# Relational graph layers on one core: engine order written out in the source, and the relation products dealt out between chunks

## The chip, the core and the metric

The kernel runs on one core of a Trainium2 chip. A core has a matrix engine, TensorE (PE in the profile, its weight loads PEld), three engines for elementwise work, VectorE (DVE), ScalarE (ACT) and GpSimd (POOL), and SyncE (SP), which here only issues transfers. Each engine takes its instructions in order; semaphores make it wait for others. SBUF is the working memory with 128 partitions, PSUM the memory that TensorE writes, in banks of 512 fp32 per partition. Transfers are issued by SP, ACT and POOL; the indirect ones, which gather rows by index, are issued by POOL.

The metric is the device time of one execution in microseconds, the median over runs, lower is better.

## The reference

6250 nodes with 256 features; 106250 edges, sorted by destination (each of 50000 pairs in both directions, and a loop at each node); 8 edge types; three relational layers, then one attention layer.

```
h = relu(layernorm(x))
for l in range(3):
    xr  = einsum('nd,rde->rne', h, W_rel[l])
    agg = segment_sum(xr[edge_type, src], dst)
    h   = relu(agg + h @ W_root[l] + bias[l])
x = x + h
h = relu(layernorm(x)) @ Wv + bv
c = leaky_relu((h @ wq + bq)[src] + (h @ wk + bk)[dst])
x = x + segment_sum(h[src] * softmax_over_dst(c), dst)
```

## The kernel before

The kernel looks at the edges and takes one of two paths; with these inputs it is `ordered_path`, which uses that edges are sorted by destination.

**Preparation.** Edges are cut into 831 chunks of 128. The nodes, then, are covered by 56 windows of consecutive chunks: 47 windows of 15 chunks (`CW`), then 9 of 14. A window's destinations fit into 128 nodes that begin at `base[t]`. The first loop (`groups`, four tiles of 128 nodes) normalizes x and writes two tables to memory: `xf[0]`, fp32 rows of h, and `tab[0]`, the same rows as three bf16 parts (high, middle, low) whose sum is the fp32 number: 768 bf16 per row. Each layer writes the next layer's `xf` and `tab`.

**A layer.** For a chunk, `gather` (L719) fetches the 128 source rows of `tab[l]` into `msg` (36 buffers). VectorE makes `hot` (L871): a row per edge with a single 1 at column 8 x (node in window) + type, over those nodes only that the chunk can reach (`ranges`, 104 to 336 columns). TensorE multiplies msg by hot (L852): for each half h of the features and each of the three parts, a weight load of 128 x 128 msg and a matmul into the PSUM banks of the window. There are four banks, two halves of 64 nodes times two halves of features, from a pool of five. A chunk that reaches over the middle needs two matmuls per weight load: 108 matmuls in a window of 15, 102 in one of 14. The last chunk of the window before is added once more with `hot_p`, 8 columns wide, for the node that is cut by the border.

**Finishing a window.** `finish_window` (L772) is called for window t-1 after chunk 2 of window t, and after the last window. It reads the window's own rows `xt` from `xf[l]` (`at_base`, L723, computes a register value from the base and the last hot, so that the load is not issued too early), copies the four banks to `ag` (three copies on ScalarE, L784, one on VectorE, L782), turns xt by two fp32 transposes into `pt` and copies it (L767, L769), and forms `po`: 16 products of `ag` with `W_rel` (L790, weight operand read with a step of 8 elements, since columns are ordered node by node with the type innermost) and two of xt with `W_root` (L793). An fp32 product appears in the profile as two instructions, so these are 32 and 4. Then come the bias (L795), relu and the split into three bf16 parts (L798, and `split`, L649), and stores to `tab[l+1]` and `xf[l+1]` (L801, L802). In the third layer, instead, x is added, stored as `xa`, normalized, turned (L767), multiplied by `Wv` (L818) and stored as a row of `hx`. `pt` and `po` have one PSUM buffer each.

**Attention.** It goes through the same windows and gathers rows of `hx` (L719 again, `head`, 48 buffers). The change does not touch it.

**What sets the order.** The kernel is written as one program; a scheduler decides in what order each engine gets its instructions, from what they need and from their buffers, and adds the semaphores. The next layer's gathers wait until all rows of its table are stored. The names that the change touches are `xf`, `base`, `hots`, `at_base`, `finish_window`, `turned_rows`, the loads at L742 to L751, and the loop at L833.

Of the kernel before, what the change touches and what calls it, by code (L numbers as in the profile page):

```python
# [10 lines left out]
F32 = mybir.dt.float32  # L11
BF16 = mybir.dt.bfloat16
I32 = mybir.dt.int32
# [416 lines left out]
def kernel(  # L430
# [52 lines left out]
    xf = [dram.tile([N + P, D], F32, name=f"xf{i}") for i in range(L)]  # L483
# [8 lines left out]
    base = keep.tile([1, NW], F32)  # L492
    last_i = keep.tile([P, 1], I32)
# [8 lines left out]
    with tc.tile_pool(name="prep", bufs=1) as prep, \  # L502
# [49 lines left out]
        for at, view, k in by_window(dst_t):  # L552
# [4 lines left out]
                              dst_t[0:1, CL + CW - 2:NC - (CW - 1):CW - 1])  # L557
        ones = prep.tile([1, P], F32)
# [109 lines left out]
    with tc.tile_pool(name="nw", bufs=3) as nw:  # L668
        zero = nw.tile([P, D], F32, bufs=1)
        nc.gpsimd.memset(zero, 0.0)  # L670
        nc.scalar.dma_start(xf[0][N:N + P, :], zero)
        for ts in groups:
            n = len(ts)
            xt = nw.tile([P, 4, D], F32, name="xt")
            whole = rows(ts[-1]) == P
            if whole:
                nc.sync.dma_start(
                    xt[:, :n, :],
                    x[ts[0] * P:(ts[-1] + 1) * P, :].rearrange("(t p) d -> p t d", p=P))
            else:  # L680
                nc.gpsimd.memset(xt, 0.0)
                for i, t in enumerate(ts):
                    nc.sync.dma_start(xt[:rows(t), i, :], x[t * P:t * P + rows(t), :])
            mv, rstd = statistics(nw, xt, n)
            for i in range(n):
                nc.vector.tensor_scalar(xt[:, i, :], xt[:, i, :], mv[:, i, 0:1],
                                        rstd[:, i:i + 1], op0=ALU.subtract, op1=ALU.mult)
            h0 = nw.tile([P, 4, D], F32, name="h0")
            nc.scalar.activation(h0[:, :n, :], xt[:, :n, :], AF.Relu)
            hml = nw.tile([P, 4, 3, D], BF16, name="hml")  # L690
            nc.scalar.copy(hml[:, :n, 0, :], h0[:, :n, :])
            nc.vector.tensor_sub(xt[:, :n, :], h0[:, :n, :], hml[:, :n, 0, :])
            nc.scalar.copy(hml[:, :n, 1, :], xt[:, :n, :])
            nc.gpsimd.tensor_sub(hml[:, :n, 2, :], xt[:, :n, :], hml[:, :n, 1, :])
            if whole:
                r0, r1 = ts[0] * P, (ts[-1] + 1) * P
                nc.sync.dma_start(xf[0][r0:r1, :].rearrange("(t p) d -> p t d", p=P),
                                  h0[:, :n, :])
                nc.sync.dma_start(tab[0][r0:r1, :].rearrange("(t p) w -> p t w", p=P),
                                  hml[:, :n].rearrange("p t s d -> p t (s d)"))  # L700
            else:
                for i, t in enumerate(ts):
                    nc.sync.dma_start(xf[0][t * P:t * P + rows(t), :], h0[:rows(t), i, :])
                    nc.sync.dma_start(tab[0][t * P:t * P + rows(t), :],
                                      hml[:rows(t), i].rearrange("p s d -> p (s d)"))

    def ordered_path():
# [23 lines left out]
        with ExitStack() as s:  # L731
            wp = s.enter_context(tc.tile_pool(name="weights", bufs=2))
            mp = s.enter_context(tc.tile_pool(name="msgs", bufs=36))
            op = s.enter_context(tc.tile_pool(name="hots", bufs=20))
# [4 lines left out]
            ops = s.enter_context(tc.tile_pool(name="ops", bufs=1, space=PSUM))  # L739

            wv_s = one.tile([P, KH, D], F32)
            nc.scalar.dma_start(wv_s, wv.rearrange("(k p) e -> p k e", p=P))  # L742
# [3 lines left out]
            for to, of in ((bv_s, bv), (wq_s, wq), (wk_s, wk)):  # L746
                nc.scalar.dma_start(to, rows_bcast(of, D))
            bq_s = one.tile([P, 1], F32)
            bk_s = one.tile([P, 1], F32)
            for to, of in ((bq_s, bq), (bk_s, bk)):  # L750
                nc.scalar.dma_start(to, rows_bcast(of, 1))  # L751
# [12 lines left out]
            def turned_rows(a: bass.AP, func):  # L764
                pt = ops.tile([P, KH, P], F32, name="pt")
                for k in range(KH):
                    nc.tensor.transpose(pt[:, k, :], a[:, k * P:(k + 1) * P], ident)  # L767
                at = rp.tile([P, KH, P], F32, name="at")
                nc.scalar.activation(at, pt, func)  # L769
                return at  # L770

            def finish_window(l: int, t: int, banks, hot, weights):  # L772

                wr, wo, bb = weights
                at = at_base(t, hot)
                xt = rp.tile([P, D], F32, name="xt")
                nc.sync.dma_start(xt, xf[l][ds(at, P), :])
                ag = ap_.tile([P, KH, 2, SEG // 2], F32, name="ag")
                for half in range(2):
                    for h in range(KH):  # L780
                        if half and h:
                            nc.vector.tensor_copy(ag[:, h, half, :], banks[half][h])  # L782
                        else:
                            nc.scalar.copy(ag[:, h, half, :], banks[half][h])  # L784
                x_t = turned_rows(xt, AF.Copy)
                po = ops.tile([P, D], F32, name="po")
                for r in range(R):
                    for h in range(KH):
                        by_r = ag[:, h].rearrange("p b (n r) -> p r (b n)", r=R)
                        nc.tensor.matmul(po, by_r[:, r, :], wr[:, h, r, :],  # L790
                                         start=(r == 0 and h == 0), stop=False)
                for h in range(KH):
                    nc.tensor.matmul(po, x_t[:, h, :], wo[:, h, :], start=False,  # L793
                                     stop=(h == KH - 1))
                nc.vector.tensor_add(po, po, bb)  # L795
                if l + 1 < L:
                    xs = rp.tile([P, D], F32, name="xs")
                    nc.scalar.activation(xs, po, AF.Relu)  # L798
                    hml = rp.tile([P, 3, D], BF16, name="hml")
                    split(hml, po, po, "relu")  # L800
                    nc.sync.dma_start(tab[l + 1][ds(at, P), :], hml.rearrange("p s d -> p (s d)"))  # L801
                    nc.sync.dma_start(xf[l + 1][ds(at, P), :], xs)  # L802
                    return
# [7 lines left out]
                nc.sync.dma_start(xa[ds(at, P), :], x1[:, 0, :])  # L811
                mv, rstd = statistics(rp, x1, 1)
                nc.vector.tensor_scalar(x1[:, 0, :], x1[:, 0, :], mv[:, 0, 0:1], rstd[:, 0:1],
                                        op0=ALU.subtract, op1=ALU.mult)
                h_t = turned_rows(x1[:, 0, :], AF.Relu)
                ph = ops.tile([P, D], F32, name="po")
                for h in range(KH):
                    nc.tensor.matmul(ph, h_t[:, h, :], wv_s[:, h, :], start=(h == 0),  # L818
                                     stop=(h == KH - 1))
                nc.vector.tensor_add(ph, ph, bv_s)  # L820
# [9 lines left out]
                nc.sync.dma_start(hx[ds(at, P), :], row)  # L830

            weights = load_weights(0)
            for l in range(L):  # L833
                nxt = load_weights(l + 1) if l + 1 < L else None
                ahead = None
                pending = None
                for t in range(NW):
                    n = sizes[t]
                    banks = [[gps.tile([P, SEG // 2], F32, name="bank") for _ in range(KH)]
                             for _ in range(2)]  # L840
                    begun = [False, False]
# [18 lines left out]
                    if ahead is not None:  # L860
                        hot = op.tile([P, R], BF16, name="hot_p", bufs=3)
                        nc.vector.tensor_scalar(hot, up[:, :R], seg_p[:, t:t + 1], None,
                                                op0=ALU.is_equal)
                        add(ahead, hot, 0, R)
                    for k in range(n):
                        c = first_c[t] + k
                        lo, hi = ranges[n][k]
                        msg = mp.tile([P, 3, D], BF16, name="msg")
                        gather(msg.rearrange("p s d -> p (s d)"), tab[l], src_t[:, c:c + 1])
                        hot = op.tile([P, WMAX], BF16, name="hot")  # L870
                        nc.vector.tensor_scalar(hot[:, :R * (hi - lo)], up[:, :R * (hi - lo)],  # L871
                                                seg[:, c:c + 1], None, op0=ALU.is_equal)
                        add(msg, hot, R * lo, R * hi)
                        ahead = msg
                        if k == 2 and pending is not None:
                            finish_window(l, *pending, weights)
                            pending = None
                    pending = (t, banks, hot)
                finish_window(l, *pending, weights)
# [116 lines left out]
```

## Time and profile before

| | |
|---|---|
| median of 3 runs, without a profiler | 4491.3 us (4487.84 to 4492.17) |
| profiled execution | 6330.7 us |
| its span | 6328.4 us |
| granted TensorE clock, mean over the span | 0.818 |
| first gather of layers 1, 2, 3 and of the attention | 146.9, 1651.9, 3142.0, 4628.9 us |
| gathers | 2493 in the layers, 831 in the attention, 0.945 us busy each |
| DMA, mean over the span | 116 GB/s |

The profile's times are those of one execution, the one with the profiler attached. It is much longer than the runs, so a row's mean duration can be taken from it, but not without care the time between rows.

```profile
PE   0687887888688788888868888888844454445545
PEld 0566666666566666666757777777733343334434
...
PEclk5788988888788888888878888888966677667767
DMA  5544444444344444444344444444422222222221
```

Each column is 1/40 of the span, each digit the busy share in tenths. The layers fill the first 29 columns, the attention the rest.

In the groups of the profile, the part after the bar is the busy time of a group in us with the mean of one in ns; after the next bar is the idle time of its engine just before it, and whose work ended that wait. "issue" there means that the engine waited for nothing that the profile shows.

### The profile page before, as it was taken

What the parts mean: (1) busy time and instruction counts of PE and PEld (TensorE: products, weight loads), DVE (VectorE), ACT (ScalarE), POOL (GpSimd) and SP (SyncE); (2) the same over time, 40 slices, a digit from 0 to 9 for tenths busy, and PEclk for the clock granted to TensorE, in tenths of its full rate; (3) what the DMA queues carried; (4) which work ended last, traced back from release to release, by engine and by line L of the source; (5) the groups of instructions that cost most, each with busy time, mean ns of one, the idle gap of its engine ahead of it and who ended that gap; (6) DMA issues with size and microseconds to landing.
All of it is one profiled execution on the core that took longest, in us unless ns stands there. A gap on an engine that the chain in (4) does not pass through costs nothing. (4 is left out here: it accounts for less than half of the span.)

```text
span 6328.4 us, 79952 instructions
## 1 busy us (share of the span) xinstructions
PE 4369.9 (69%) x29260; PEld 3685.4 (58%) x29260; DVE 2154.2 (34%) x6241; ACT 1153.1 (18%) x2566; POOL 3175.4 (50%) x3411
## 2 busy tenths in 40 slices
PE   0687887888688788888868888888844454445545
PEld 0566666666566666666757777777733343334434
DVE  5222322223232222323223333333323433334434
ACT  2011111111011111111101111111123333333333
POOL 2555555555355555555355555555444444444443
PEclk5788988888788888888878888888966677667767
DMA  5544444444344444444344444444422222222221
GB/s 181 150 130 129 134 128 131 129 124 136 114 130 128 129 132 132 131 130 135 103 137 134 134 134 135 133 135 138 123 71 74 71 73 78 76 73 73 78 75 53
DMA packets 327774, 732.72 MB, mean 116 GB/s; under 512 B 65165, under 2 KB 181059, under 8 KB 327372
## 3 DMA queue, kind: packets, MB, share of 16 engines
q0 software_dynamic: 199536, 599.93, 34.4%
q1 hardware_dynamic: 117512, 118.48, 5.8%
q10 hardware_dynamic: 10324, 9.11, 0.5%
q8 instruction: 232, 3.80, 0.3%
q14 instruction: 170, 1.39, 0.1%
HBM read 652.42 MB, written 74.88 MB: 115 GB/s over the span
## 5 line engine op out<-in xcount | busy, mean ns | idle before, releaser
L719 POOL DMA_INDIRECT msg<-tab,src_t x2493 | 2355.8, 945 | 2062.7 <-PE bank L852 1060.1
L852 PE MATMUL bank<-hot,msg 128*128 128x104 bf16 (+16 forms) x17982 | 1725.4, 252 | 582.1 <-issue 416.9
L852 PEld LDWEIGHTS <-msg 128*128 128x128 bf16 x18972 | 1418.5, 102 | 896.7 <-issue 699.0
L790 PE MATMUL po<-wr,ag 128*128 128x256 f32 x5376 | 1533.4, 446 | 183.8 <-issue 165.4
L790 PEld LDWEIGHTS po<-wr,ag 128*128 128x128 f32 x5376 | 1381.2, 335 | 327.0 <-issue 226.5
L871 DVE TENSOR_SCALAR hot<-up,seg 128x104 bf16<-128x104 f32 (+10 forms) x2493 | 1017.0, 431 | 1398.9 <-PE bank L852 972.0
L719 POOL DMA_INDIRECT head<-hx,src_t x831 | 785.5, 945 | 895.6 <-PE po L945 452.8
L920 PE MATMUL pq<-ident,qm 128*128 128x128 f32 x886 | 221.9, 342 | 679.4 <-ACT qm L918 293.4
L784 ACT COPY ag<-bank 128x512 f32<-128x512 f32 x504 | 284.9, 587 | 1887.8 <-PE bank L852 1085.3
L920 PEld LDWEIGHTS pq<-ident,qm 128*128 128x128 f32 x886 | 130.6, 158 | 753.8 <-ACT qm L918 328.0
L795 DVE TENSOR_TENSOR po<-po,bb 128x256 f32<-128x256 f32 x168 | 72.7, 433 | 1270.7 <-PE po L793 1247.2
L945 PE MATMUL po<-head,ex 128*128 128x256 f32 x1772 | 457.3, 416 | 42.6 <-issue 30.6
L945 PEld LDWEIGHTS po<-head,ex 128*128 128x128 f32 x1772 | 368.3, 214 | 111.3 <-issue 41.3
L924 DVE TENSOR_REDUCE tops<-pq 128x1 f32<-128x512 f32 x224 | 153.0, 683 | 553.3 <-ACT c L923 340.2
L918 ACT ACTIVATE qm<-other,head 128x128 f32<-128x128 f32 x886 | 298.7, 394 | 119.5 <-issue 95.9
L938 PE MATMUL pe<-ident,c 128*128 128x128 f32 x886 | 190.6, 388 | 152.3 <-ACT c L933 142.7
L938 PEld LDWEIGHTS pe<-ident,c 128*128 128x128 f32 x886 | 162.5, 205 | 174.4 <-ACT c L933 158.5
L911 DVE TENSOR_SCALAR other<-up,loc 128x128 f32<-128x128 f32 x831 | 256.9, 340 | 11.1 <-ACT qm L918 10.8
L923 ACT ACTIVATE c<-pq,sm 128x512 f32<-128x512 f32 x224 | 150.1, 683 | 572.6 <-remote 472.2
L798 ACT ACTIVATE xs<-po 128x256 f32<-128x256 f32 x112 | 42.9, 383 | 988.8 <-DVE po L795 980.1
L818 PE MATMUL po<-wv_s,at 128*128 128x256 f32 x224 | 111.8, 652 | 159.6 <-ACT at L769 156.0
L782 DVE COPY ag<-bank 128x512 f32<-128x512 f32 x168 | 116.1, 691 | 273.6 <-remote 128.7
(135 smaller groups left out, 1844.2 us busy)
## 6 DMA issues: line engine op xcount, KB each, us to landing
msg<-tab,src_t POOLq DMA_INDIRECT x2493
xt<-xf SPq DMA_DIRECT2D x168, 128.0 KB
tab<-hml SPq DMA_DIRECT2D x112, 192.0 KB
xf<-xs SPq DMA_DIRECT2D x112, 128.0 KB
head<-hx,src_t POOLq DMA_INDIRECT x831
tab<-hml SPq DMA_DIRECT2D x12, 768.0 KB
hx<-row SPq DMA_DIRECT2D x56, 128.5 KB
xa<-x SPq DMA_DIRECT2D x56, 128.0 KB
```

The source lines that it names most:

```text
L719: nc.gpsimd.indirect_dma_start(out=to, out_offset=None, in_=table[:N, :], in_offset=bass.IndirectOffsetOnAxis(ap=index, axis=0))
L784: nc.scalar.copy(ag[:, h, half, :], banks[half][h])
L790: nc.tensor.matmul(po, by_r[:, r, :], wr[:, h, r, :], start=(r == 0 and h == 0), stop=False)
L852: nc.tensor.matmul(banks[b][h][:, a - b * SEG // 2:z - b * SEG // 2], w, hot[:, a - lo:z - lo], start=(not begun[b] and s_ == 0), stop=Fal ...
L871: nc.vector.tensor_scalar(hot[:, :R * (hi - lo)], up[:, :R * (hi - lo)], seg[:, c:c + 1], None, op0=ALU.is_equal)
L911: nc.vector.tensor_scalar(other, up[:, :P], refs[j][1], None, op0=ALU.not_equal)
L918: nc.scalar.activation(qm, other, AF.Identity, scale=MASKED, bias=refs[j][0][:, D:HX])
L920: nc.tensor.transpose(pq[:, i, :], qm, ident)
L923: nc.scalar.activation(to, flat, AF.Identity, scale=SLOPE, bias=k2)
L924: nc.vector.tensor_reduce(tops[:, g:g + 1], flat, AX.X, ALU.max)
L938: nc.tensor.transpose(pe[:, i, :], c_t[:, j * P:(j + 1) * P], ident)
L945: nc.tensor.matmul(po, ex[:, i, :], refs[j][0][:, :D], start=(j == 0), stop=(j == len(refs) - 1))
```

## The change

- A call of `manual_schedule` at the start of the layers: each engine's instructions stay in the order in which the source gives them.
- `xf` is gone. The window's own rows are read from `tab[l]` as three bf16 parts, at chunk 4 of the window, at an address from `base_i`, an integer copy of `base`. They are turned by six bf16 matmuls with an identity `ident_b` that add the three parts up.
- `hot` has 10 buffers for 20 and is made five chunks ahead (`make_hot`).
- A half's two banks are allocated when its first chunk comes, and are copied out by ScalarE as soon as its last chunk is summed (`evacuate`). The copy reorders: `ag` is now [128, 2, type, node], so a product's weight operand is contiguous, and the read from PSUM has a step of 8 elements.
- `finish` is a generator. After each chunk it is resumed once, and issues its next piece: the turn; then 12 pieces of the 18 products (8 in the last layer); then bias, split and store, or in the last layer the norm, the turn, the product with `Wv` and the row, one piece each. A window's pieces are issued during the next window's chunks; what is left after the last chunk of a layer is run through at once, window after window.
- The loads for the head (`wv_s` and so on) are issued at the start of the third layer instead of the first.

```diff
-            op = s.enter_context(tc.tile_pool(name="hots", bufs=20))
+            s.enter_context(tc.manual_schedule())
+            op = s.enter_context(tc.tile_pool(name="hots", bufs=10))
...
+            def evacuate(banks, half: int, ag: bass.AP):
+                for h in range(KH):
+                    nc.scalar.copy(ag[:, h, :, half * (P // 2):(half + 1) * (P // 2)],
+                                   banks[half][h].rearrange("p (n r) -> p r n", r=R))
+            def finish(l: int, at, xt: bass.AP, ag: bass.AP, weights, t: int):
+                wr, wo, bb = weights
                 pt = ops.tile([P, KH, P], F32, name="pt")
                 for k in range(KH):
-                    nc.tensor.transpose(pt[:, k, :], a[:, k * P:(k + 1) * P], ident)
...
+                    for i in range(3):
+                        nc.tensor.matmul(pt[:, k, :], xt[:, i, k * P:(k + 1) * P], ident_b,
+                                         start=(k == 0 and i == 0), stop=(k == KH - 1 and i == 2),
+                                         skip_group_check=True)
+                x_t = rp.tile([P, KH, P], F32, name="x_t")
+                nc.scalar.copy(x_t, pt)
+                yield
+                last = l + 1 == L
+                parts = STEPS - (6 if last else 2)
+                todo = [(r, h) for r in range(R) for h in range(KH)] + [(R, h) for h in range(KH)]
+                po = ops.tile([P, D], F32, name="po")
+                done = 0
+                for i in range(parts):
+                    upto = len(todo) * (i + 1) // parts
+                    for r, h in todo[done:upto]:
+                        if r < R:
+                            nc.tensor.matmul(po, ag[:, h, r, :], wr[:, h, r, :],
+                                             start=(r == 0 and h == 0), stop=False,
+                                             skip_group_check=True)
                         else:
...
+                            nc.tensor.matmul(po, x_t[:, h, :], wo[:, h, :], start=False,
+                                             stop=(h == KH - 1), skip_group_check=True)
+                    done = upto
+                    yield
                 nc.vector.tensor_add(po, po, bb)
-                if l + 1 < L:
-                    xs = rp.tile([P, D], F32, name="xs")
-                    nc.scalar.activation(xs, po, AF.Relu)
+                if not last:
                     hml = rp.tile([P, 3, D], BF16, name="hml")
                     split(hml, po, po, "relu")
                     nc.sync.dma_start(tab[l + 1][ds(at, P), :], hml.rearrange("p s d -> p (s d)"))
-                    nc.sync.dma_start(xf[l + 1][ds(at, P), :], xs)
+                    yield
                     return
...
-                nxt = load_weights(l + 1) if l + 1 < L else None
+                nxt = load_weights(l + 1) if l + 1 < L else load_head()
...
+                for i in range(AHEAD):
+                    make_hot(i)
+                for i, (t, k) in enumerate(order):
...
+                    msg = mp.tile([P, 3, D], BF16, name="msg")
+                    gather(msg.rearrange("p s d -> p (s d)"), tab[l], src_t[:, i:i + 1])
+                    if i + AHEAD < len(order):
+                        make_hot(i + AHEAD)
+                    hot, hot_p = hots[i]
+                    if hot_p is not None:
+                        add(ahead, hot_p, 0, R)
+                    add(msg, hot, R * lo, R * hi)
+                    ahead = msg
+                    if 0 in halves and (k == n - 1 or R * ranges[n][k + 1][0] >= SEG // 2):
+                        evacuate(banks, 0, ag)
+                    if k == n - 1:
+                        evacuate(banks, 1, ag)
+                    if unfinished:
+                        if next(unfinished[0], "done") == "done":
+                            unfinished.pop(0)
+                    if k == 4:
+                        at = nc.sync.value_load(base_i[0:1, t:t + 1], min_val=0,
+                                                max_val=N - P if t < NW - 1 else N - 1)
+                        xt = rp.tile([P, 3, D], BF16, name="xt")
+                        nc.sync.dma_start(xt.rearrange("p s d -> p (s d)"), tab[l][ds(at, P), :])
+                    if k == n - 1:
+                        unfinished.append(finish(l, at, xt, ag, weights, t))
+                for f in unfinished:
+                    for _ in f:
+                        pass
```

## The prediction

> **What bounds the kernel now.** The profiled execution took 6330.7 us (span 6328.4); the runs without a profiler have a median of 4491.3. That gap comes first, since a sum against the wrong one of the two is worth nothing. I read the page's engine rows and costliest groups, then a table of two stretches, then the timelines of GpSimd and of the layer ends. The chain of waits has four pieces and 1 us, so it carries nothing.
>
> ```profile
> PE 4369.9 (69%) x29260; PEld 3685.4 (58%) x29260; DVE 2154.2 (34%) x6241; ACT 1153.1 (18%) x2566; POOL 3175.4 (50%) x3411
> L719 POOL DMA_INDIRECT msg<-tab,src_t x2493 | 2355.8, 945 | 2062.7 <-PE bank L852 1060.1
> L790 PE MATMUL po<-wr,ag 128*128 128x256 f32 x5376 | 1533.4, 446 | 183.8 <-issue 165.4
> ```
>
> In the profile GpSimd waits for TensorE: the 36 message buffers are full, and the sums set the pace. The two stretches are about one window each, the first after the last gather of a layer, the second among gathers (columns: length, busy time of PE, PEld, DVE, ACT, POOL, granted clock, DMA):
>
> ```profile
> 1599.40:1616.10 16.70, 16.70 (x150) 16.06 (x148) 7.26 (x21) 3.08 (x7) 0.00 (x0) 1.00 0.12 36
> 2009.00:2035.80 26.80, 22.15 (x150) 18.12 (x151) 7.79 (x21) 3.07 (x7) 14.09 (x16) 0.81 0.45 128
> ```
>
> The same 150 matmuls take 16.7 us without a gap and 26.8 with gaps whose releaser is "issue", at a clock of 0.81. If 26.8 held in the unprofiled runs, 168 windows alone would be 4502 us, more than the whole kernel. So most of these gaps belong to the profiled execution, and TensorE's own need is near 16.7 us for a window of 14 chunks. A 15th chunk adds 6 matmuls of about 0.08 us: 17.2. GpSimd's need is read where nothing holds it:
>
> ```profile
> 1594.76 0.95 POOL L719 DMA_INDIRECT msg<-tab,src_t  x1 [0.30 <-issue]
> 1651.88 0.94 POOL L719 DMA_INDIRECT msg<-tab,src_t  x1 [56.17 <-DMA tab<-hml]
> 1653.13 0.95 POOL L719 DMA_INDIRECT msg<-tab,src_t  x1 [0.30 <-issue]
> ```
>
> One gather each 1.2475 us (0.945 busy and 0.30 after it): 18.7 us for 15, 17.5 for 14, more than TensorE needs. All 2493 + 831 = 3324 gathers: 4147 us. The first starts at 146.9. That leaves 4491.3 - 4147 - 146.9 = 197 us of the median. The layer ends (worked out below) take about 69, the last window's chain some 30, and the attention loop, whose last undisturbed windows were 17.5 to 19.6 us long, up to 85 above its gathers. 184 of 197 is close enough: **without the profiler the layers run at GpSimd's gather pace**, TensorE 8% below it. This is inferred from two times and a cadence, not seen.
>
> **The change, part by part.** It keeps every gather. So what can move is the start, the three layer ends, and the margin of TensorE.
>
> *Start.* 13 stores of xf[0] go (6.4 MB). At the 315 GB/s of the busiest slice that is at most 20 us, at least nothing: between two rounds SP waits for GpSimd's subtraction (L694), not for these stores. Nearest row: the loads issued at 101.8 were first used at 107.55, behind two table stores, the xf stores of 93.2 mostly drained. I take 2. The head's six loads (139.3 to 142 on ACT) no longer run beside the last table store, which took 8.0 us from issue (138.95) to the first gather; undisturbed it was 2.6 (below). 0 to 5.4; I take 2, since this store is of 106 rows and slower alone. Start: -4.
>
> *TensorE in a window.* Columns: start, length, ...
>
> ```profile
> 1599.86 0.38 PE L767 MATMUL pt<-ident,xt 128*128 128x128 f32 x2
> 1600.08 7.95 PE L790 MATMUL po<-wr,ag 128*128 128x256 f32 x32
> 1607.86 1.03 PE L793 MATMUL po<-wo,at 128*128 128x256 f32 x4
> 1608.73 0.47 PE L852 MATMUL bank<-hot,msg 128*128 128x176 bf16 x4
> ```
>
> L790 runs at (1607.86 - 1600.08)/32 = 0.243 us, L793 at (1608.73 - 1607.86)/4 = 0.217: same product, but L790 loads weights with a stride of 8 elements (338 ns against 190). The new ag is contiguous: -32 x 0.026 = -0.8. Turning x by 6 bf16 matmuls instead of two fp32 ones: 6 x 0.055 - 0.22 = +0.1. Dealing out breaks the products into 12 pieces, each behind a bf16 matmul: a 190 ns load of fp32 weights after about 100 ns of matmul leaves 0.09 open, 12 times: +1.1 (0 if loads are always early enough, 2.3 if none overlaps). So 16.7 becomes 17.1, 17.2 becomes 17.6; in the last layer (4590.13 to 4607.21 between transposes, 17.1) 17.5 and 18.0. All stay below 18.7; the nine windows of 14 chunks stand level with their 17.5. **Nothing gained, nothing lost**, while GpSimd sets the pace.
>
> *Waits of the fixed order.* DVE now waits in place for the window's last product, with five hots ready: 5 x 1.25 = 6.2 us of cover for the 2.5 us of L795 to L654 (1641.36 to 1643.86). SP waits for hml before it may load the next xt, due several chunks later. GpSimd's queue holds gathers only, except one of x at the very end. ACT has four copies for three (+0.6) and no xs (-0.4), 3 of 18.7 us busy; DVE loses the copy L782 (-0.7) and L726. Nothing behind these is late, and each costs at most its cover's shortfall, which I see nowhere.
>
> *ScalarE's strided read: row and rule.* The row: a copy of 512 contiguous elements, 0.587 us, so two copies 1.2. The Trainium skill, "SBUF — State Buffer", Door 1: The DMA port swizzle, says PSUM has 8-byte cachelines and that non-contiguous access slows matmuls significantly. No row of this trace reads a bank with a stride of 8 fp32. Estimate from that page: half of each line wasted, 2 x 0.587 = 1.17 per copy, 2.3 for two. Between the last sum and the first product of ag TensorE now has hot_p 0.15, a chunk 0.33, the turn 0.35 and a chunk 0.44, 1.3 us, or 2.5 if it waits for two gathers. By the row nothing is lost; by the rule 1.0 per window if TensorE is behind, nothing at the gathers' pace. I take the row; the rule speaks against the change and prices a rival.
>
> *Layer ends.* This is where I put the cost. finish() needs 14 resumptions and one more that only ends it. A window of 15 chunks gives 15, one of 14 gives 14, so each of the nine short windows at a layer's end slips one: at the last chunk finish(54) has had 6 of its 14. Before, it was done at k == 2. What is left is run ahead of finish(55), in TensorE's order.
>
> ```profile
> 1632.35 8.11 PE L790 MATMUL po<-wr,ag 128*128 128x256 f32 x32
> 1640.30 1.03 PE L793 MATMUL po<-wo,at 128*128 128x256 f32 x4
> 1641.36 0.43 DVE L795 TENSOR_TENSOR po<-po,bb 128x256 f32<-128x256 f32 x1 [8.20 <-PE po L793]
> 1643.44 0.42 DVE L654 TENSOR_TENSOR hml<-po,hml 128x256 bf16<-128x256 f32 x1 [0.44 <-ACT hml L653]
> 1643.89 0.33 SPq L801 DMA_DIRECT2D tab<-hml  x1
> ...
> 3139.38 0.33 SPq L801 DMA_DIRECT2D tab<-hml  x1
> ...
> 3142.01 0.95 POOL L719 DMA_INDIRECT msg<-tab,src_t  x1 [50.81 <-DMA tab<-hml]
> ```
>
> From the last sum to the next gather: 1632.1 to 1651.9 = 19.8, 3127.6 to 3142.0 = 14.4, 4607.3 to 4628.9 = 21.6. With 5.5 for the last gather to land and be summed, less one pace, these are 24, 19 and 26: the 69 above. After: 7 of 12 parts left, 21 half-products x 0.217 = 4.5, then 2.9 until the one po buffer is free, less 1.2 for faster products and the missing L798: +6. At the first end the table store took 8.0 us against 2.6 at the second, because the weights' loads had started at 1640.5; now they queue on ACT behind the split: -4. At the second the head's loads come there instead: +1.5. In the last layer 3 of 8 parts are left, 14 x 0.217 = 3.0, then the norm and the wv product through one po buffer (4616.6 to 4624.65, less the first's end): 7.1, less 0.9: +9. Ends: +2, +7.5, +9 = +18.5.
>
> Sum: 4491.3 - 4 + 18.5 = **4506 us**, slower by 0.3%. Against the profiled execution the same -4 and +18.5 apply; its windows, set by TensorE's gaps, could move by far more either way, and I derive nothing for the median from that.
>
> **Rivals.** (B) *TensorE's stalls count without the profiler too.* For it: the rows put 1060 us of GpSimd's wait on TensorE, and 52 on DVE's ag copy. Against it: the 4502 us above, and 184 of 197 us being spoken for without it. If the attention's 85 us are such stalls and the new order ends them: 4506 - 85 = 4421. Below 4147 + 147 + 69 + 30 = 4393 it can't go unless the cadence itself is the profiler's. (C) *TensorE becomes the bound: it is slower by more.* In its fixed order it waits for ScalarE's second half before the first product. It decides once the new stall and the breaks add over 1.1 us to a window of 15 (18.7 - 17.6). With the rule's 1.0 on 17.6 and breaks at 0.15 instead of 0.09 (+0.7), 19.3 against 18.7 in 141 windows and 18.8 against 17.5 in 27: 85 + 35 = 120, giving 4625. For it: the margin is thin, and the last layer has less. Against: 36 buffers absorb a late moment, and a stall at the gathers' pace has 2.5 us of cover. (D) *It does not pay at the ends*: the slip costs less, start and ends cancel, 4491. I hold this inside the forecast's own range.
>
> **Numbers.** Forecast, with D in it, 0.60, own range 4480 to 4535; B 0.15; C 0.25. I call 0.2% (9 us) the least that this kernel's runs (4487.8 to 4492.2) tell from no change. Of the forecast's 0.60 some 0.36 lie above 4500, 0.20 within, 0.04 below. So slower 0.36 + 0.25 = 0.61, same 0.20, faster 0.19. For 8 in 10, half of B and most of C belong in: 4425 to 4625.
>
> **What would show it.** Right: gathers still 1.25 us apart; from the last gather of a layer to the next layer's first, products of two windows one after the other; L790's products at 0.217 with loads of 190 ns; ScalarE's copies near 0.59. Copies near 1.2 with TensorE waiting for ag: C. A median under 4450 would make the gather cadence, or the reading that TensorE's gaps are the profiler's, wrong.

## The result, and the profile after

The changed kernel takes **4521.9 us** (median of four runs, 4519.0 to 4527.0) against 4489.6 for the kernel before beside it (4486.6 to 4492.2): ratio 1.0074, interval 1.0056 to 1.0091, so about 33 us slower. A repetition (e8) gave 1.0077 (1.0063 to 1.0090). The forecast was 4506, with a range of 4480 to 4535; its sign and its range hold, its sum is 16 us short, so that the loss is twice the one forecast.

Four of the experiments below (e4 to e7) ran on a chip on which the kernel before takes 6317.7 us, so their times are set only against runs on that chip.

The profiled execution of the changed kernel took 4520.3 us, as long as the runs. From its page, the engine row and groups (after the first bar busy us and mean ns of one, after the second the idle time before and its releaser):

```profile
PE 3775.3 (84%) x29932; PEld 3129.4 (69%) x29932; DVE 2030.9 (45%) x5907; ACT 1179.9 (26%) x2622; POOL 3177.1 (70%) x3411
...
L717 POOL DMA_INDIRECT msg<-tab,src_t x2493 | 2357.4, 946 | 855.0 <-issue 398.1
...
L797 PEld LDWEIGHTS po<-wr,ag 128*128 128x128 f32 x5376 | 898.0, 191 | 66.8 <-DVE hml L655 6.2
...
L772 ACT COPY ag<-bank 128x512 f32<-128x512 f32 x672 | 361.6, 591 | 1915.7 <-PE bank L896 1903.7
```

POOL's idle time in the layers is now mostly the 0.30 us that follow each gather: 2493 times 0.30 are 748 of the 855 us, whatever releaser the row names. The weight loads of the products, now contiguous, went from 338 to 191 ns. ScalarE's copies, now with a stride of 8 elements in PSUM, take 591 ns; the contiguous ones took 587.

Since the profiled execution of before, at 6330.7 us, was not one like the runs, the kernel before was profiled again (e0_before, 4496.6 us). The difference can then be read off the gathers alone: from the first to the last of a stretch, and from the last of one to the first of the next (us, from the traces of the profiled executions):

| | first gather | layer 1 | end 1 | layer 2 | end 2 | layer 3 | end 3 | attention | after the last |
|---|---|---|---|---|---|---|---|---|---|
| before (e0) | 146.7 | 1040.1 | 25.9 | 1040.3 | 20.8 | 1048.2 | 63.5 | 1047.6 | 61.2 |
| changed | 120.7 | 1037.8 | 31.3 | 1037.6 | 28.8 | 1075.5 | 80.3 | 1045.6 | 60.9 |
| difference | -26.0 | -2.3 | +5.4 | -2.7 | +8.0 | +27.3 | +16.8 | -2.0 | -0.3 |

These sum to +24.2; the spans differ by 24.0 (4518.4 - 4494.4). The 8 us missing to the 32.4 of the runs are mostly the gathers' own pace: their median distance is 1.254 us in e0 and 1.251 in the changed kernel's trace, so an undisturbed layer needs 1040 us there and 1037.8 here, some 2.5 us more in each of four stretches. The chip alone does not set this pace: the traces of e10 and e11, from one chip, have 1.251 and 1.254. What does, no run tells. **The start gained 26 us, the ends lost 30, and the third layer, in which no step of the prediction put anything, lost 27 us as read, and 30 with the two paces set equal.**

### The profile page after: what moved, and what is told of

It is laid out like the page before. It is cut to its first block, busy times and chain, and to the rows that moved or that the text cites. A ratio compares the mean times of both kernels' runs of the same rounds, so it can differ in the third digit from the quotient of the medians.

```text
span 4518.4 us, 81585 instructions
## 1 busy us (share of the span) xinstructions
PE 3775.3 (84%) x29932; PEld 3129.4 (69%) x29932; DVE 2030.9 (45%) x5907; ACT 1179.9 (26%) x2622; POOL 3177.1 (70%) x3411
## 5 line engine op out<-in xcount | busy, mean ns | idle before, releaser
L896 PEld LDWEIGHTS <-msg 128*128 128x128 bf16 x18972 | 1397.8, 98 | 687.2 <-DMA msg<-tab,src_t 311.2
L797 PE MATMUL po<-wr,ag 128*128 128x256 f32 x5376 | 1494.9, 392 | 6.7 <-DVE hml L655 4.9
L864 DVE TENSOR_SCALAR hot<-up,seg 128x104 bf16<-128x104 f32 (+10 forms) x2493 | 953.0, 430 | 647.4 <-PE bank L896 643.1
L797 PEld LDWEIGHTS po<-wr,ag 128*128 128x128 f32 x5376 | 898.0, 191 | 66.8 <-DVE hml L655 6.2
L772 ACT COPY ag<-bank 128x512 f32<-128x512 f32 x672 | 361.6, 591 | 1915.7 <-PE bank L896 1903.7
L970 PE MATMUL pq<-ident,qm 128*128 128x128 f32 x886 | 202.0, 320 | 171.1 <-ACT qm L968 169.9
L968 ACT ACTIVATE qm<-other,head 128x128 f32<-128x128 f32 x886 | 299.5, 397 | 146.1 <-issue 117.7
L801 PE MATMUL po<-wo,x_t 128*128 128x256 f32 x672 | 173.2, 380 | 0.0
L652 ACT ACTIVATE hml<-po 128x256 bf16<-128x256 f32 x112 | 43.0, 384 | 489.1 <-DVE po L805 398.5
L975 DVE SCALAR_TENSOR_TENSOR c<-pq,k_n,c 128x512 f32<-128x512 f32 x224 | 164.7, 735 | 0.0
L991 ACT COPY ex<-pe 128x512 f32<-128x512 f32 x112 | 64.5, 576 | 352.4 <-PE pe L988 352.4
```

The lines of the kernel that those rows point to most:

```text
L772: nc.scalar.copy(ag[:, h, :, half * (P // 2):(half + 1) * (P // 2)], banks[half][h].rearrange("p (n r) -> p r n", r=R))
L797: nc.tensor.matmul(po, ag[:, h, r, :], wr[:, h, r, :], start=(r == 0 and h == 0), stop=False, skip_group_check=True)
L896: nc.tensor.matmul(banks[b][h][:, a - b * SEG // 2:z - b * SEG // 2], w, hot[:, a - lo:z - lo], start=(not begun[b] and s_ == 0), stop=Fal ...
L968: nc.scalar.activation(qm, other, AF.Identity, scale=MASKED, bias=refs[j][0][:, D:HX])
L970: nc.tensor.transpose(pq[:, i, :], qm, ident)
L975: nc.vector.scalar_tensor_tensor(to, flat, k1, to, op0=ALU.add, op1=ALU.max)
```

## The experiments

Four questions were tried: what a profile of before shows that is as long as the runs, what the slip at the layer ends is worth, what slows the third layer, and what moved the start.

| run | kernel | median, us | ratio to before on the same chip |
|---|---|---|---|
| e0_before | before | 4496.6 (one run) | (before: 4495.1) |
| e1_no_slip | changed, no slip | 4524.3 | 1.0063 (1.0050 to 1.0077) |
| e2_norm_gap | changed, one chunk more between norm and turn | 4504.8 | 1.0023 (1.0014 to 1.0031) |
| e3_both | e1 and e2 | 4502.4 | 1.0015 (1.0009 to 1.0022) |
| e4_own_norm | changed, norm in its own tile | 5813.5 | 0.9192 (before: 6317.7) |
| e5_own_norm_gap | e3 and own tile | 5799.6 | 0.9171 (before: 6317.7) |
| e6_before_own_norm | before, norm in its own tile | 6416.3 | 1.0158 (before: 6317.7) |
| e7_xf_back | changed, stores to xf[0] again | 5873.5 | 0.9295 (before: 6317.7) |
| e8_after_again | changed | 4522.7 | 1.0077 (1.0063 to 1.0090) |
| e9_own_norm_gap | as e5 | **4438.3** | **0.9886** (0.9871 to 0.9901) |
| e10_own_norm_only | as e4 | 4474.4 | 0.9946 (0.9933 to 0.9960) |
| e11_before_own_norm | as e6 | 4475.4 | 0.9948 (0.9934 to 0.9962) |

### A profile of before that is like the runs

> The kernel before, unchanged, looked at once more, since its profile took 6331 us and its runs 4490. Theory (gather pace): in a profile of about 4490 us the layers run one gather each 1.25 us, 1037 to 1045 us from first to last gather of each layer, the third included; from last to first gather 24, 19 and about 30 us; TensorE's windows keep a lag of a few us behind the gathers in all three layers. Rival (the scheduler's order already has TensorE stalls): at least one layer takes over 1060 us.

The first two layers are as expected, a gather each 1.25 us and ends of 25.9 and 20.8. The third, at 1048.2, fits neither expectation: its sums fall behind the gathers by 3 us at first and 41 in its last window (each window's first sum against its first gather), which the 36 buffers mostly absorb, so that the lag is paid at its end, 63.5. TensorE's waits in the middle of the third layer say for what (us in total, times, longest):

```profile
PE pt L767 <- DVE x L813: 32.3, 41, 2.8
```

The kernel before, too, waits once a window for the normalized rows. The forecast took the third layer for one more at the gathers' pace.

### The slip

In `finish`, the last resumption only ends the generator. e1 takes the `yield` away that stands ahead of that, in both branches, so that a window of 14 chunks is done within the next window's 14 chunks:

```diff
                     nc.sync.dma_start(tab[l + 1][ds(at, P), :], hml.rearrange("p s d -> p (s d)"))
-                    yield
                     return
...
                 nc.sync.dma_start(hx[ds(at, P), :], row)
-                yield
```

> The changed kernel, without the resumption that only ends a window's pieces, so that a window of 14 chunks has room for all 14. Theory (slip): the next-to-last window is done before the last chunk; each of the first two layer ends is 6 us shorter (31.3 to 25, 28.8 to 23), the third about 10 (80 to 70), time 4522 - 22 = 4500. Rival (the ends are long for another reason, the table's store and the weights): no change, 4522.

Ends 1 and 2 fell by 3.7 and 3.9 us (31.3 to 27.6, 28.8 to 24.9) and end 3 by 6.3, but the third layer grew from 1075.5 to 1085.1, of which some 2.5 us are the pace of e1's gathers (1.254): its nine short windows, most of which had left a part of their work behind and taken 17.4 to 20.2 us, now mostly take 20.1 to 20.6 and do it all. In all about 5 us, the intervals of the two ratios overlapping, so the gain in time is not shown. The shorter ends show that the slip is there; it costs at most a quarter of what was expected, since the third layer takes its part back.

### The third layer: spacing, and a store in the norm's way

TensorE's windows in the third layer are mostly 19.7 to 20.8 us long in the changed kernel, against the 18.7 that 15 gathers take; after 27 windows the 36 buffers are used up (TensorE is 45 to 48 us behind) and GpSimd waits. In the middle of that layer TensorE is busy for 769.26 of 850 us (first line: stretch, length, busy time, instructions, granted clock, DMA), and the wait of the second line is nearly all the rest:

```profile
2400.00:3250.00 850.00, 769.26 (x6841) 0.99 0.64 182
```

```profile
PE pt L827 <- DVE x L822: 80.3, 42, 2.8
```

One window of the changed kernel (start, length; in brackets the wait just before, and its releaser):

```profile
2801.59 0.43 DVE L805 TENSOR_TENSOR po<-po,bb 128x256 f32<-128x256 f32 x1 [7.10 <-PE po L801]
2802.06 0.42 DVE L818 SCALAR_TENSOR_TENSOR x<-po,x 128x256 f32<-128x256 f32 x1
...
2802.51 0.35 SPq L819 DMA_DIRECT2D xa<-x  x1
...
2803.76 0.16 DVE L665 RECIPROCAL rstd<-rstd 128x1 f32<-128x1 f32 x1 [0.36 <-ACT rstd L664]
2804.49 0.41 DVE L822 TENSOR_SCALAR x<-x,mv,rstd 128x256 f32<-128x256 f32 x1 [0.57 <-DMA xa<-x]
...
2805.05 0.41 PE L827 MATMUL pt<-ident,x 128*128 128x128 f32 x2 [1.62 <-DVE x L822]
```

The order is fixed, so TensorE stands at the turn (L827) until VectorE has the norm; over the 56 windows that is 112 us. Between the last product and the turn it has 24 matmuls to do, about 2 us. In the kernel before (e0) the scheduler had put 56 there, and the wait was shorter. First the changed kernel, then the one before:

```profile
2801.39 2.04 PE L896 MATMUL bank<-hot,msg 128*128 128x48 bf16 x24
```

```profile
2796.01 3.74 PE L852 MATMUL bank<-hot,msg 128*128 128x176 bf16 x56
...
2800.69 0.41 PE L767 MATMUL pt<-ident,x 128*128 128x128 f32 x2 [0.94 <-DVE x L813]
```

The first thought was that the pieces are too close. e2 puts one more chunk between the norm and the turn and, so that a window still fits, deals the products out over one piece fewer:

```diff
-                parts = STEPS - (6 if last else 2)
+                parts = STEPS - (7 if last else 2)
...
                                         op0=ALU.subtract, op1=ALU.mult)
                 yield
+                yield
                 pt = ops.tile([P, KH, P], F32, name="pt")
```

> The changed kernel with one more chunk between the norm and the turn that needs it, in the third layer, and one piece fewer for the products. Theory (TensorE waits in place for the norm, 1.9 us in each window of the third layer): TensorE's window falls from 19.7 to about 17.9 us, below the 18.7 of the gathers; the lag at the third layer's last chunk falls from 47 us to about 6, the layer takes 1038 and its end 41 us less together; time 4522 - 79 + 2 for slips with less room = about 4445 if both the 38 us in the layer and the 41 at its end go, since they are the same lag seen twice only if GpSimd's stall were not also counted; 4481 if just one of them. Rival (the products with Wv and their turn are simply too much for TensorE): no change, 4522.

> Both edits together: no slip, and one more chunk between norm and turn. Theory: the effects add, 22 us less than the run with the gap alone, and below the kernel before (4490) in any case: 4420 to 4460. Rival (with the gap the third layer slips anyway or the ends don't matter once the lag is gone): no better than the gap alone.

Both gained, e2 0.5% and e3 hardly more, and both missed what was expected: the third layer is still 1061.2 and 1065.7 us long. e2's VectorE in one window shows why:

```profile
2805.41 0.16 DVE L665 RECIPROCAL rstd<-rstd 128x1 f32<-128x1 f32 x1 [0.36 <-ACT rstd L664]
2806.64 0.41 DVE L822 TENSOR_SCALAR x<-x,mv,rstd 128x256 f32<-128x256 f32 x1 [1.07 <-DMA xa<-x]
```

The norm has all its numbers at 2805.57 and starts at 2806.64. What ends the wait is the store of `xa`, issued at 2804.11, 2.5 us earlier: L822 writes over the very rows (`x1`) that this store is reading, so it has to wait for the store to end. A DMA that nobody needs soon stood in TensorE's path through a reused buffer. The edit gives the norm a tile of its own:

```diff
-                nc.vector.tensor_scalar(x1[:, 0, :], x1[:, 0, :], mv[:, 0, 0:1], rstd[:, 0:1],
+                x2 = rp.tile([P, D], F32, name="x2")
+                nc.vector.tensor_scalar(x2, x1[:, 0, :], mv[:, 0, 0:1], rstd[:, 0:1],
                                         op0=ALU.subtract, op1=ALU.mult)
...
-                    nc.tensor.transpose(pt[:, k, :], x1[:, 0, k * P:(k + 1) * P], ident)
+                    nc.tensor.transpose(pt[:, k, :], x2[:, k * P:(k + 1) * P], ident)
```

It was tried on the changed kernel (e4, e10), on e3 (e5, e9), and, with the same lines, on the kernel before (e6, e11). The first three runs fell on the chip where the kernel before takes 6317.7 us:

> The changed kernel with one edit: the third layer's norm writes a tile of its own, where it overwrote in place the rows that the store of xa is still reading. Theory A (the store is in the third layer's chain): the norm's 48 us of waiting for that store over 56 windows goes, TensorE's 112 us of waiting for the norm falls to about 65, a third-layer window falls from 19.7 to about 19.0 us, and layer and end together lose 25 to 48 us: 4475 to 4500 us. Theory B (the window is set by TensorE's own work and ScalarE's copies): TensorE's wait moves to another name and the time stays within 5 us of the changed kernel's 4522 to 4527.

> e3_both (no slip, one more chunk between norm and turn; 4502 us) with the norm in a tile of its own. Theory A: TensorE's wait ahead of the turned rows, 62 us over 43 windows in e3_both, nearly goes, the third layer falls to the gathers' pace (about 1043 us from first to last gather) and its end from 70 to about 40 us: 4440 to 4465 us, clearly below the kernel before. Theory B: the wait in e3_both is for the selection masks queued on VectorE and not for the store; then at most 10 us are gained, 4492 to 4502.

> The kernel before with the same one edit (norm in a tile of its own). Theory A: its third layer lags too (to 41 us behind the gathers at the end) and the same store is in its chain (22 us in 29 windows); without it the lag at the end falls to about 20 us and the time to 4465 to 4480 us. Theory B (the scheduler had already put other work there): within 5 us of the kernel before.

There they tell nothing of the question: from the second window of the first layer on TensorE is some 45 us and more behind, and the windows of every layer are mostly 20 to 26 us long (to 32 in e6), whatever the third adds. (e6 is even slower than before there, with a third layer of 1529 us against 1422 in the first profile of before; the cause was not looked for.) Hence the repetitions:

> The changed kernel as it is, run beside the kernel before. On a chip where the kernel before takes about 4490 us: 1.0074 again, 4515 to 4535 us. On a chip where it takes about 6300 us and TensorE stalls for 0.3 to 1 us with no wait that the trace shows: the gathers there wait for TensorE in all three layers, so fewer and shorter TensorE instructions count in full, and the changed kernel needs 5830 to 5880 us (e7_xf_back's 5873 less the 26 us that the stores put back cost it, or e4_own_norm's 5814 plus 15 to 50), ratio about 0.925.

> The kernel of e5_own_norm_gap again. On a chip where the kernel before takes about 4490 us, theory A (the store of xa in the norm's way): third layer at the gathers' pace, 1043 us from first to last gather, its end 40 us instead of 70, 4440 to 4465 us. Theory B (masks queued on VectorE): 4492 to 4502 us. On a chip where it takes about 6300 us: 5790 to 5810 us as before, and nothing is told apart.

e8 repeats the result. e9 takes 4438.3 us, 2 us below the range of theory A and far from theory B, 1.1% faster than the kernel before. Its third layer is 1038.0 us from first to last gather, the pace of the first two (1037.8 and 1037.5), and its end 40.5. The same steps of a window in its trace:

```profile
2812.91 0.16 DVE L665 RECIPROCAL rstd<-rstd 128x1 f32<-128x1 f32 x1 [0.36 <-ACT rstd L664]
2813.11 0.41 DVE L822 TENSOR_SCALAR x<-x,mv,rstd 128x256 f32<-128x256 f32 x1
...
2813.67 0.41 PE L828 MATMUL pt<-ident,x 128*128 128x128 f32 x2 [0.55 <-DVE hot_p L860]
```

The norm follows 0.04 us after the reciprocal, with no bracket, and TensorE's wait at the turn is 0.55 instead of 1.62. In the same stretch of 850 us TensorE now does 7282 instructions for 6841:

```profile
2400.00:3250.00 850.00, 816.67 (x7282) 1.00 0.67 190
```

```profile
PE pt L828 <- DVE hot_p L860: 23.0, 40, 0.8
...
PE pt L828 <- DVE x L822: 3.4, 6, 0.7
```

The releaser is named `hot_p`, VectorE's next instruction after the norm, but the turn needs the norm alone, and starts 0.15 us after its end here as in the changed kernel; so these waits, too, are put down to the norm. Which part did how much:

> The kernel of e4_own_norm again (the changed kernel, norm in a tile of its own, slip and spacing as they are), to split the 84 us between the changed kernel (4522.7) and e9_own_norm_gap (4438.3). Where the kernel before takes about 4490 us: if the parts add, the store is worth 84 less the 20 us that spacing and slip gave alone in e3_both, so 4455 to 4460 us. If both have to be gone before TensorE's window fits under the gathers' 18.7 us, the store alone leaves a window near 19.0 us, a third layer of about 1045 us and an end of about 60 us: 4465 to 4485 us.

> The kernel of e6_before_own_norm again (the kernel before with the norm in a tile of its own). Where the kernel before takes about 4490 us: its third layer ends 41 us behind the gathers, and the norm's wait for the store was 22 us of it; theory A 4465 to 4475 us, so that with the same repair on both sides the change is worth 25 to 35 us (4438 against this). Theory B: within 5 us of the kernel before, since its scheduler put other work into that wait.

The store alone (e10) brings the changed kernel from 1.0077 to 0.9946 (ratios from two chips), about 59 us at 4490. TensorE's wait for the norm falls from 112 to 67 us over the 56 windows. Its windows are 19.2 us, still over 18.7; they fall 35 us behind instead of using up the buffers, so that the gathers keep their pace (1037.6) and the lag is paid at the end (69.3). Spacing and slip alone (e3) bring 0.6%, 28 us; together (e9) 1.9%, 86. Within the intervals the parts add; with the tile in place, spacing and slip were not tried one by one. At 4490 us e10's ratio is 4466, at the lower edge of its second expectation (4465 to 4485), and its interval, 4460 to 4472, reaches the first (4455 to 4460): the time does not tell them apart. The window of 19.2 is nearly what the second says; its layer of 1045 and end of 60 came out as 1037.6 and 69.3, with the same sum. In the kernel before (e11) the same edit is worth 0.5%, about 23 us, as its theory A has it: its window falls to 19.1 us, its lag at the end to 28. There the scheduler had put five of VectorE's masks (L871) between the steps of that chain, and still some of TensorE's wait was left. With this repair alone on both sides the two kernels are level (0.9946 and 0.9948), although the changed one starts its gathers 27 us earlier; with spacing and slip mended too it comes out ahead (0.9886 against 0.9948).

### The start

The first loop's SP queue: loads of x (L677, L678), stores of the two tables. Start, length of the issue, and how many, from e0_before:

```profile
75.73 2.43 SPq L677 DMA_DIRECT2D xt<-in_x_dram  x3
86.51 0.38 SPq L697 DMA_DIRECT2D xf<-h  x1
92.45 0.37 SPq L699 DMA_DIRECT2D tab<-hml  x1
92.91 2.13 SPq L697 DMA_DIRECT2D xf<-h  x2
99.02 2.44 SPq L699 DMA_DIRECT2D tab<-hml  x2
101.56 2.46 SPq L677 DMA_DIRECT2D xt<-in_x_dram  x3
```

and from the changed kernel:

```profile
77.47 0.46 SPq L678 DMA_DIRECT2D xt<-in_x_dram  x1
85.14 0.38 SPq L698 DMA_DIRECT2D tab<-hml  x1
85.61 0.46 SPq L678 DMA_DIRECT2D xt<-in_x_dram  x1
```

Before, SP goes in rounds of three groups, 25.8 us each: the next three loads stand behind the last of three table stores. Without the stores to `xf[0]` the scheduler puts most loads directly behind one table store, and the rounds overlap. This loop is outside `manual_schedule`. e7 puts the stores back, into a tensor that nobody reads:

```diff
             if whole:
                 r0, r1 = ts[0] * P, (ts[-1] + 1) * P
+                nc.sync.dma_start(xf[0][r0:r1, :].rearrange("(t p) d -> p t d", p=P),
+                                  h0[:, :n, :])
```

> The changed kernel with the stores of the fp32 rows of layer 0 put back into the first loop, read by nobody. Theory A (these stores in SyncE's order held the next loads back): first gather back from 120.7 to about 147 us, time +26 to about 4548 us. Theory B (the earlier start comes from the weights of the head no longer being loaded there): first gather stays below 125 us, time within 5 us.

The first gather is at 146.1 us and SP's queue is in rounds of three loads again (50.7, 76.6, 102.4). So the 26 us come from those stores. The head's loads were absent from the start in e7 too, so they are not the cause. Its time, on the chip of e4 to e6, can't be set against the expected 4548; against e4 (5813.5) it is 60 us slower, of which the start is 25, and e4 has the norm in its own tile besides.

## Why the prediction was right, and where it was not

**What bounds the kernel.** Right for layers 1 and 2 and for the attention: at 1.2475 to 1.251 us per gather a layer of 831 takes 1037.8, and TensorE mostly follows 3 to 6 us behind, before and after. The sum that supported this, 184 of 197 us, came out by luck: it had 69 us for the ends, 30 for the last window's chain and 85 for the attention, where e0 has some 107, 60 and 12 on the same count, and 22 more in the layers. It hid that the third layer of the kernel before already lagged. That the gaps in the first profile belong to "the profiled execution" was half right: they are not the profiler's, since nine of the fourteen profiled executions here are as long as undisturbed runs, and those of e4 to e7 as long as the runs beside them; but they don't belong to the runs of 4490 either. The last section returns to them.

**Terms of the sum**, from the segments above:

| step | predicted | measured |
|---|---|---|
| start | -4 (0 to -25) | -26 |
| TensorE's window in layers 1 and 2 | 0 | 0 |
| third layer | 0 | +27 to +30 |
| layer ends | +2, +7.5, +9 | +5.4, +8.0, +16.8 |

*Start.* The step priced the bytes of the stores and kept SP's order, saying that between two rounds SP waits for GpSimd's subtraction, not for these stores. So it does, in that order; the removal changed the order itself. The 2 us for the head's loads were not gained: from the last table store to the first gather it is 8.4 us (112.26 to 120.66) against 8.1.

*Third layer.* This is the step that failed: "All stay below 18.7 ... Nothing gained, nothing lost" for a last layer of 17.5 and 18.0, and, of the fixed order's waits, "Nothing behind these is late, and each costs at most its cover's shortfall, which I see nowhere". VectorE, SP, GpSimd and ScalarE were gone through; TensorE's own wait for the norm was not. The work was sized well enough: 769.26 us in 42 windows is 18.3 for a predicted 18.0. The 1.9 of wait on top makes 20.2. The stretch of the first profile from which the last layer's 17.1 was read (4590.13 to 4607.21) already shows the norm held by the store:

```profile
4601.88 0.41 DVE L813 TENSOR_SCALAR x<-x,mv,rstd 128x256 f32<-128x256 f32 x1 [0.59 <-DMA xa<-x]
```

TensorE had 50 matmuls to do in the meantime there (3.43 us) and turned at 4602.44 without a wait. The new order leaves it 24. Rival C had the mechanism in general ("in its fixed order it waits"), but put it at ScalarE's second half and in all layers; it is VectorE's norm, in one. The measured 30 us are a quarter of C's 120.

*Layer ends.* The mechanism is right, as e1 shows, and is seen in the two windows' products one behind the other at the first end, with the wait for the one `po` buffer between them:

```profile
1163.47 4.48 PE L797 MATMUL po<-wr,ag 128*128 128x256 f32 x20
...
1171.13 8.86 PE L797 MATMUL po<-wr,ag 128*128 128x256 f32 x32 [1.99 <-DVE hml L655]
```

20 half-products in 4.48 against a predicted 21 in 4.5. At the first end the -4 for the weights was wrong: they are issued at 1182.35, still beside the last table store at 1183.1, and store to gather takes 6.6 us against 7.5 in e0. The second end is right to 0.5, the head's loads there +1.7 (4.3 against 2.6) for a predicted +1.5; but the slip, priced at +6 at each of these ends, gave back only 3.7 and 3.9 when e1 took it away, so the sum is better than its parts. The third had 9 for the products and the norm; the work after the last sum grew by 11.6 (21.6 to 33.2), and 5 come from the larger lag.

*The small ones.* L797's products are 0.217 apart when dealt out, as said, but for the first pair behind each break (0.25); a break costs about 0.04, not 0.09. ScalarE's strided read: the row was right (591 ns). The Trainium skill, "SBUF — State Buffer", Door 1: The DMA port swizzle, speaks of matmuls where it says that non-contiguous PSUM access slows them; the estimate of 1.17 us, which carried this over to a copy, does not hold for ScalarE here.

So two terms that were mis-sized by 22 us (start) and 27 to 30 us (third layer) nearly cancelled, by luck; what is left of the 16 us is mostly the ends, 30 for a predicted 18.5.

## What to carry to other kernels

When an order is fixed by hand, go through every wait of the engine that is near the bound itself, not only through those of the engines that it releases; a wait that the scheduler had covered with other work is then covered only as far as the source does it. Look at what ends each wait in the chain: a result computed in place over a tile that a store is still reading makes the store part of the chain, and one more small tile takes it out. And removing a transfer from a loop that is scheduled automatically can be worth more than its bytes (26 us here, where the bytes alone came to at most 20), since the order of what remains is made anew.

## What the runs showed of the hardware that was not expected

**The same kernel at 4490 and at 6318 us.** On one chip nine runs of the kernel before took 6303.9 to 6336.7 us, as its first profile did (6330.7); in all the other runs 4486 to 4506. The gathers' own pace is the same there (1.251 and 1.254 us, median). TensorE is what differs: in places it issues a few instructions, then none for about half a microsecond, with nothing in the trace to wait for. The 900 us from 1300 on hold 5786 of its instructions in e4_own_norm, at a granted clock of 0.91, and 7496 in the changed kernel's trace, at 1.00. From e4_own_norm, TensorE in the second layer:

```profile
1607.66 0.21 PE L897 MATMUL bank<-hot,msg 128*128 128x120 bf16 x1 [0.40 <-issue]
...
1608.38 0.32 PE L897 MATMUL bank<-hot,msg 128*128 128x104 bf16 x3 [0.51 <-issue]
```

The granted clock over the span is 0.858 there (0.927 for the changed kernel on its chip), and 0.70 against 0.80 in the attention, where both have the same work and need 1616 and 1046 us. On that chip TensorE paces all three layers, and the change as a whole pays: with the stores to `xf[0]` put back, so at the start of before, it is still 7.0% faster (e7_xf_back), the first layer 1252.9 us against 1441.6 in e6, whose first layer is that of before. TensorE stalling without a profiler is what rival B supposed, though not for the runs of 4490 us. Whether it is the chip or its condition while these runs were taken, why TensorE stalls, and whether the clock is cause or sign of it, no run here tells; the changed kernel without an edit was not run there.

**A store of 128 KB held its source for 2 to 2.5 us.** From the issue of `xa`'s 128 KB on SP to the norm that waits for it: 2802.51 to 2804.49 in the changed kernel, 2804.11 to 2806.64 in e2.
